# A vision layer in one kernel: softmax sums of two tiles of keys in one pass, with the exponentials added on VectorE

## The chip, the cores and the metric

The kernel runs on one core of one Trainium2 chip. The metric is the time of one execution on the device, in microseconds (us). PE is TensorE, ACT is ScalarE, DVE is VectorE, POOL is GpSimd, SP is SyncE, which here only starts DMAs. PEld is the loading of weights into TensorE.

## The reference, cut to what matters

Sixteen images of 512 x 512 become 1024 tokens each of 256 channels; one layer of attention and one of a mixture of networks follow.

```python
h = tokens(x)                                    # patches @ W + b
q, k, v = split(layernorm(h) @ w_qkv)            # 8 heads of 32
k = sum over f = 1..256 of a_f*sin(f*k) + b_f*cos(f*k)
dots = einsum('bhqd,bhkd->bhqk', q, k) * 32**-0.5
out = einsum('bhqk,bhkd->bhqd', softmax(dots), v)
h = h + out @ w_out + b_out
h = h + networks(layernorm(h))                   # shared MLP + 2 of 4 gated experts
```

All is fp32. The change touches the softmax and the product with `v`.

## The kernel before, in words

The work is cut into rounds. A round makes the transformed keys of four groups of a head pair (the sum over frequencies) and, two rounds behind, one *attention*: two heads against 512 queries, over all 1024 keys. There are 16 images x 4 head pairs x 2 halves of the queries = 128 attentions, each over `NT` = 8 tiles of 128 keys, so 1024 tiles of keys.

For one tile of keys, `kc`:

- **S** (`score`, L1134): two matmuls make the scores of 128 keys against 512 queries for both heads in a PSUM tile `sT` of 128 x 1024 fp32. It comes from the pool `big`, which has two buffers that rotate.
- `exponential` (L1149): ACT takes the exponential from PSUM into an SBUF tile `es`, of which there are `NES` = 5. The big buffer is free after that.
- **W** (`weigh`, L1167): TensorE in four column tiles of 32. Four matmuls multiply `es` with the values `v` (numerators, columns 0 to 255 of the PSUM tile `av`) and four with `ones32`, all ones (denominators, columns 256 to 511). Each matmul leaves two records in the profile. `av` collects over the eight tiles; then `normalize` (L1191 to L1208) takes the reciprocal on DVE, multiplies, and frees `av` for the next attention.

For the keys, SP loads tiles `w` (L951), DVE spreads tiles `f` (L991), POOL multiplies both with integer frequencies (L1006, "turn"), ACT takes sines (L1016), **M** (`mix`, L1036) mixes eight row and column tiles of PE into the second kind of tenant of `big`, `kan`; DVE multiplies it with `f` (L1050, "prod"), and **R** (`add_up`, L1069) adds up. ACT needs one table for sines and another for exponentials, so a round has twelve sines in a row, then eight exponentials, with other small steps between.

Everything else (tokens, norms, keys, queries, values, output projection, networks) is written as four chains of small steps, 0 to 3. A chain's matmul step uses one of two PSUM side banks. The step `values` (L643 to L669) multiplies two tiles of tokens with `wv`; ACT copies the result into the SBUF tile `v`, and for the last head pair into `last`, from where POOL copies it later (`last_values`).

The order of PE's work is written out as strings, `ORDER`: S, M, R, W are the fixed steps, a digit is the next step of that chain. While the program is built, a planner with a cost for each step (`put`, `begin`, `lay_fixed`, `others`) lays the steps of the other engines between: at each point the step that could begin first goes first. The engines then run these queues in order. The strings have 3840 letters; 240 of them make up one image and are repeated eleven times.

Lines that matter: L297 to L306 are the helpers that the chains' matmuls use (L301 whole array, L304 in column tiles, L310 transposes); L548 adds the token bias on DVE; L589 to L599 reduce the angles on DVE, partly in place in PSUM (L594).

Of the kernel before, what the change touches and what calls it, by code (L numbers as in the profile page):

```python
# [11 lines left out]
FP = mybir.dt.float32  # L12
# [6 lines left out]
P = 128  # L19
E = 256  # L20
NPAIR = 4
# [41 lines left out]
KINDS = {"M": "mix", "R": "red", "S": "score", "W": "av"}  # L63
COLUMNS = (128, 32)
ORDER = (
    "333333313133100003000030M0M000MMR3R3M3M",
    "303RMM3MR330M3R3M03MSSRSSWSSWSSWWWW0MWM",
    "WMMRSSSRSWSSWSSW0WWWWMMW3MMRSSRSSWSSWSSW0WW0MMWWWMMRSSRSSWSSWSSW0WWMWWMWMRMSSSWSSWSSWSRW"
    "WWWWMMMMRSSSWSSWSSWSRWWWWW0M0MM0RMS0SSWSSWSWSWSWWW3W3MR13M3MMRSSRSSWSS1SSWWWW3WMWWM3RMS1"
    "SS1SS0SSWWWMS3WR3WWWWM0MMRMS0SS1SR1SSWW1S1SW0W1WW1MMW1W1MM1SSRWSS0SS1WSSWW10RWMWWW1MM10M"  # L70
    "S1SSRWSWR1SS1WSS1W1MMWWMMWW0SS1R1SS1WW1SS1SSW1WRW1WMMW3WMMRS1SS1SW1SS3SSW1WR1WWWWWMM13MM"
    "1RSS0SS0SS0SWWWSWWWR3MMW1WS10S1RSS1S3MMWSS3WRWWSW1WWMW31MM0SS1SSRMS1SSWWWSWR3WWWW3MM131M"
    "S1RSSWWMWSSR3S1S3S1WWW01M1WW1MM0RSS1SWSSWMS1SSWRWW01MW1WWMM101SSRMW1SSWWSS1RSS101MMWWWWW"
    "MS3SSWRMWSS1S01SSW1RW0W3MMWWRWSS131SS1MMWWSS1SSRWWW1WWW101",
    (
        "MM10RMM1SS01SS1SS1WWSS1WWWRWWWMM10MMRS3S1SS1SSWWWSS3RWWWW1W3MM0RMM3SSRSWWWSS1SS1S3WWWMMW"
        "3W311MSRM1WS1S3SWWS3S1SSRW1W0WMM1WWRMM10SS1SS1WW1SS0SSWWRW1WWW0MM10MM1SS1RRWWSS0S1SWSS1W"
        "WWWWMM1S0SRWSSWMMWS1S31SSWRW3WW1WMM3MMR1SS1SS1SSWWWSS1WRWW1WW101"
    )
    * 11,  # L80
    "MM1MM1SSRRWWS1S0SS0SSWWW130MMWW1WRM1MS1",
    "3SSRWWWSS31SS1SW1WWWWMM3RM1S0SSWSS1SSWWMSWR3WWM3WWMM13S1SR1MSWWRS3S1SWS3SWWW01MM1WW10MMR"
    "1SS1SSRWSS1S1WWS0WWWWWMM101MM1SS1RS1SRSSWWWSS01WWMMWWWMS1SSWSSRW0SS1S1WMWWR1WWMM10W1MMR1"
    "SS1SSWWSS1SSWWWR1WM1WW101MM10S1MR1SSWRS1SWSSWS1WWMMWWWRMM1SS0SSWWSSWSSRWWW1WW1M0M1RSS1SS"
    "WSSWSMWSM1WWRWM1W1WMM1RM1SS1SSWWSS1SSWR1W1W1W1MM1WWR1SM1SS1SSWWSSWS1MWWRWMWWM1SS1SWSMSRM"
    "WS1SS1WR1WWW1WW1MM1M1RSS1SWWSS1SSWSWMWW1RW1MM1RW1MM1SSR1SSWWSS1WWSSWWWW1SSSWSSWWSSWSSWWW"
    "W1SS1SS1SWWSSWWWWWW11110110111110000101000100101001000100",
)

@with_exitstack  # L90
def plain_path(ctx: ExitStack, tc: tile.TileContext, a: dict, out: bass.AP, verdict: bass.AP):
# [173 lines left out]
    def begin(engine, deps):  # L265

        if any(d not in done for d in deps):
            return None
        return max([clock[engine]] + [done[d] + LAG for d in deps])
# [138 lines left out]
    def others(limit):  # L408

        soonest = None  # L410
        again = True
        while again:
            again = False
            soonest = None
            for engine in (SP, POOL, ACT, DVE):
                while True:
                    settle()
                    best = min(heads(engine), default=None)
                    chain = min(wanting(engine), default=None)
                    if chain and (  # L420
                        best is None
                        or chain[0] < best[0]
                        or (chain[0] == best[0] and best[2] not in ("prod", "keys"))
                    ):
                        at, lay_it = chain[0], lambda c=chain[1]: step(c)
                    elif best:
                        at, lay_it = best[0], lambda q=best[2]: lay(engine, q)
                    else:
                        break
                    if at > limit:  # L430
                        soonest = at if soonest is None else min(at, soonest)
                        break
                    lay_it()
                    again = True
        return soonest

    def lay_fixed(kind):

        cost, deps, key, action = queues[PE][kind][0]
        user = USERS.get(kind)  # L440
        at = begin(PE, deps + (bigs[-2:-1] if user else []))

        def lay_it():
            queues[PE][kind].pop(0)
            clock[PE] = done[key] = at + cost + retile(TILINGS.get(KINDS[kind]))
            if user:
                bigs.append((user, *key[1:]))
            action()

        return at, lay_it  # L450
# [192 lines left out]
    def values(b):  # L643

        if b > 0:
            yield "av", 2 * NPAIR * b - 3, NT - 1
            yield "all values", b - 1
        last = images[b]["last"] = kup.tile([P, NT, 2, HD], FP, tag="last", name="last")
        for t0 in range(0, NT, 2):
            yield ANY  # L650
            ps = side_tile("v").rearrange("p (t e) -> p t e", t=2)
            for t in range(2):
                for c in range(2):
                    matmul(
                        out=ps[:, t, :],
                        lhsT=hnT[:, c, ts(t0 + t, P)],
                        rhs=wv[:, c, :],
                        start=(c == 0),
                        stop=(c == 1),
                    )  # L660
            yield ACT, 0.62
            src = ps.rearrange("p t (i s d) -> p t i s d", s=2, d=HD)
            for s in range(2):
                nc.scalar.copy(
                    v[:, ds(t0, 2), 0 : NPAIR - 1, ds(HD * s, HD)],
                    src[:, :, 0 : NPAIR - 1, s, :],
                )
            nc.scalar.copy(last[:, ds(t0, 2), :, :], src[:, :, NPAIR - 1, :, :])
        mark("values", b)  # L669

    def last_values(b):
        if b > 0:
            yield "av", 2 * NPAIR * b - 1, NT - 1
        yield POOL, 0.7
        for s in range(2):
            nc.gpsimd.tensor_copy(
                v[:, :, NPAIR - 1, ds(HD * s, HD)], images[b]["last"][:, :, s, :]
            )
        mark("all values", b)

    def gate_weights(ps):
# [463 lines left out]
    def exponential(att, kc):  # L1145
        def action():
            now["table"] = AF.Exp
            es = exps[kc] = esp.tile([P, 1024], FP, tag="es", name="es")
            nc.scalar.activation(es, scores.pop(kc), AF.Exp, scale=SCALE)  # L1149

        deps = [("score", att, kc)]
        old = att * NT + kc - NES
        if old >= 0:
            deps.append(("av", *divmod(old, NT)))
        put(ACT, "fixed", 0.99, deps, ("exp", att, kc), action)

    def weigh(att, kc):

        p = att // 2

        def action():
            if kc == 0:
                acc[0] = avp.tile([P, 512], FP, tag="av", name="av")
            es = exps.pop(kc)
            for half in range(2):
                for i in range(4):
                    nc.tensor.matmul(  # L1167
                        out=acc[0][ts(i, HD), ts(half, 256)],
                        lhsT=ones32 if half else v[:, kc, p % NPAIR, ts(i % 2, HD)],
                        rhs=es[:, ds(512 * (i % 2) + 256 * (i // 2), 256)],  # L1170
                        start=(kc == 0 and half == 0),
                        stop=(kc == NT - 1),
                        skip_group_check=True,
                    )

        deps = [("exp", att, kc)]
        if kc == 0:
            b, i = divmod(p, NPAIR)
            deps.append(("all values" if i == NPAIR - 1 else "values", b))
            if att > 0:  # L1180
                deps.append(("norm", att - 1))
        put(PE, "W", 0.86, deps, ("av", att, kc), action)

    def normalize(att):
        p, qb = divmod(att, 2)
# [44 lines left out]
    def feed(c, *gens):  # L1230
        chains[c]["gens"] += gens

    for name in ("prod", "keys", "norm", "spread"):
        queues[DVE][name] = []
    queues[SP]["source"] = []
    for j in range(XBUFS):
# [33 lines left out]
    for rd in range(B * RI + 2):  # L1270
        groups = range(GS * rd, min(GS * rd + GS, total))
        att = rd - 2
        attends = 0 <= att < ATT
        for g in groups[::2]:
            first = g == groups[0]
            for i, j in ((0, 0), (0, 1), (1, 0), (1, 1), (0, 2), (1, 2)):
                sine(g + i, j, TABLE if first and i == j == 0 else 0.0)
            mix(g)
            mix(g + 1)
            add_up(g // 2)  # L1280

        def table():
            now["table"] = AF.Exp
            nc.scalar.activation(spare[:, 1:2], spare[:, 0:1], AF.Exp)

        put(ACT, "fixed", TABLE + 0.2, [], ("table", rd), table)
        for kc in range(NT) if attends else ():
            score(att, kc)
            exponential(att, kc)
            weigh(att, kc)  # L1290
    with tc.manual_schedule():
        run()
# [746 lines left out]
```

## Time and profile before

| what | value |
|---|---|
| time, median of 3 runs | 3930.66 us (3921.68 to 3933.11) |
| profiled execution, its own time | 3924.07 us |
| its span, from the first to the last instruction | 3922.5 us |
| mean granted TensorE clock | 0.994 |
| busy: PE, PEld | 3810.0, 1948.9 us |
| busy: ACT, POOL, DVE | 3263.0, 3193.6, 2531.7 us |
| DMA | 916.51 MB, mean 234 GB/s |

The profile is one execution. A group of instructions is a line of the kernel, an engine, an operation, and what is written and read (`out<-in`); after the bar come the total busy time in us, the mean of one in ns, and the idle time of the engine just before them with what ended it. A row of waits says which line waited for which, the total in us, how often, and the longest. Matmuls are pipelined and their ends are modelled: the time of one is read from start to start, and a PE that reads as busy can be waiting.

### The profile page before, as it was taken

Reading aid. Unit: us, or ns where it says so; the run is one execution under the profiler, and the core shown is the slowest. Engines: PE = TensorE matmul, PEld = TensorE weight load, DVE = VectorE, ACT = ScalarE, POOL = GpSimd, SP = SyncE. Lnnn points to the kernel's source line nnn. Section 1 sums busy time; section 2 is a strip of 40 time slices with the busy share of each in tenths; the row PEclk is TensorE's granted clock in tenths of the full one; section 3 lists DMA queues with packets and bytes.
Section 4 is the critical chain, followed back from the end, with each engine's and each line's share of the span. In section 5 each row is a group of like instructions: output and inputs, shape, how many; then the busy total and the mean of one; then the engine's idle time right before and its main releaser. Section 6 shows DMA issues by size and latency. Waiting matters only on the chain.

```text
span 3922.5 us, 102737 instructions
## 1 busy us (share of the span) xinstructions
PE 3810.0 (97%) x40337; PEld 1948.9 (50%) x40337; DVE 2531.7 (65%) x4075; ACT 3263.0 (83%) x3939; POOL 3193.6 (81%) x2328
## 2 busy tenths in 40 slices
PE   7899999999999999999999999999999999999998
PEld 4334454554545555455454545545455454544444
DVE  4656757667675766757667675776767767576652
ACT  2788888888888888888888888888888888888983
POOL 3998878788788878879788788878879888888860
PEclk9999999999999999999999999999999999999999
DMA  7987968888787888979889788798878889788860
GB/s 228 281 261 217 278 192 245 259 226 258 220 257 225 237 264 224 259 216 256 235 233 265 212 257 247 224 265 224 262 218 255 247 229 265 216 245 235 221 170 18
DMA packets 587615, 916.51 MB, mean 234 GB/s; under 512 B 58828, under 2 KB 177524, under 8 KB 587124
## 3 DMA queue, kind: packets, MB, share of 16 engines
q1 hardware_dynamic: 580880, 906.98, 80.6%
q8 instruction: 321, 5.26, 0.6%
q10 hardware_dynamic: 6244, 2.88, 0.3%
q14 instruction: 170, 1.39, 0.1%
HBM read 758.64 MB, written 150.99 MB: 232 GB/s over the span
## 4 chain that ended last, share of the span: by engine, by line
PE 66%; DMA 13%; ACT 8%; POOL 5%; DVE 4%; issue 3%; SPq 2%; ACTq 0%; POOLq 0%; DVEq 0%
PE av L1167 17%; PE sT L1134 10%; PE kan L1036 8%; DMA w<-ud 7%; PE red L1069 4%; PE e1p L301 3%; PE tok L301 3%; ACT w L1016 3%; POOL w L1006 3%; PE e3p L301 2%; PE tok L304 2%; DMA k<-kd 2%; PE s1p L301 2%; PE e1p L304 2%; ACT f L1016 2%
## 5 line engine op out<-in xcount | busy, mean ns | idle before, releaser
L1006 POOL TENSOR_TENSOR w<-w,lane 128x1024 int32<-128x1024 int32 x1024 | 1923.6, 1895 | 406.9 <-DMA w<-ud 275.7
L1149 ACT ACTIVATE es<-sT 128x1024 f32<-128x1024 f32 x1024 | 1014.3, 1022 | 357.3 <-PE sT L1134 312.2
L1016 ACT ACTIVATE w<-w 128x1024 f32<-128x1024 int32 x1024 | 1013.4, 1046 | 67.5 <-POOL w L1006 64.3
L1006 POOL TENSOR_TENSOR f<-f,lane 128x1024 int32<-128x1024 int32 x512 | 970.2, 1895 | 102.0 <-DVE f L991 84.8
L1134 PE MATMUL sT<-q,k 128*128 128x512 f32 x2048 | 707.6, 454 | 42.9 <-DMA k<-kd 13.4
L1050 DVE TENSOR_TENSOR f<-kan,f 128x1024 f32<-128x1024 f32 x512 | 605.2, 1214 | 203.1 <-ACT f L1016 116.3
L991 DVE STREAM_SHUFFLE f<-src 128x1024 int32<-128x1024 int32 x512 | 681.3, 1370 | 0.4
L1167 PE MATMUL av<-es,v 128*32 128x256 f32 x8192 | 638.8, 383 | 3.5 <-DVE rc L1208 2.6
L1167 PE MATMUL av<-es,ones 128*32 128x256 f32 x8192 | 630.9, 379 | 0.0
L1036 PE MATMUL kan<-w,coef 64*32 64x512 f32 x8192 | 540.1, 598 | 18.8 <-ACT w L1016 12.6
L1016 ACT ACTIVATE f<-f 128x1024 f32<-128x1024 int32 x512 | 519.0, 1046 | 4.1 <-POOL f L1006 4.1
L1134 PEld LDWEIGHTS sT<-q,k 128*128 128x128 f32 x2048 | 351.2, 190 | 340.0 <-issue 146.0
L1167 PEld LDWEIGHTS av<-es,v 128*32 128x32 f32 x8192 | 235.5, 109 | 343.2 <-issue 236.9
L1167 PEld LDWEIGHTS av<-es,ones 128*32 128x32 f32 x8192 | 267.2, 110 | 176.4 <-issue 1.4
L1191 DVE RECIPROCAL rc<-av 128x256 f32<-128x256 f32 x128 | 224.8, 1756 | 169.5 <-PE av L1167 169.5
L1036 PEld LDWEIGHTS kan<-w,coef 64*32 64x32 f32 x8192 | 129.1, 105 | 313.9 <-issue 133.4
L1069 PE MATMUL red<-f,pack 128*32 128x512 f32 x2048 | 271.0, 602 | 0.0
L301 PE MATMUL tok<-wt,x 128*128 128x256 f32 x768 | 182.1, 389 | 22.1 <-DMA w1s<-in_sW 12.5
L1016 ACT ACT_TABLE_LOAD x128 | 164.2, 1283 | 17.7 <-DMA w<-ud 15.5
L304 PE MATMUL tok<-wt,x 128*32 128x256 f32 x3072 | 178.0, 380 | 0.6 <-DVE h L548 0.6
L301 PEld LDWEIGHTS tok<-wt,x 128*128 128x128 f32 x768 | 147.4, 194 | 57.9 <-DMA w1s<-in_sW 12.4
L513 ACT ACTIVATE hn<-h,less,rstd 128x256 f32<-128x256 f32 x256 | 140.7, 591 | 39.8 <-POOL less L505 39.0
(148 smaller groups left out, 4269.5 us busy)
## 6 DMA issues: line engine op xcount, KB each, us to landing
w<-ud SPq DMA_DIRECT2D x2048, 256.0 KB
q<-qd SPq DMA_DIRECT2D x512, 128.0 KB
k<-kd SPq DMA_DIRECT2D x128, 512.0 KB
x<-in_xT SPq DMA_DIRECT2D x128, 384.0 KB
ud<-u SPq DMA_DIRECT2D x64, 512.0 KB
ud<-ui SPq DMA_DIRECT2D x64, 512.0 KB
src<-ud SPq DMA_DIRECT2D x512, 64.0 KB
qd<-qhi SPq DMA_DIRECT2D x64, 256.0 KB
```

Source lines behind the costliest of these rows:

```text
L301: nc.tensor.matmul(out=out, lhsT=lhsT, rhs=rhs, start=start, stop=stop)
L304: nc.tensor.matmul(out=out[ts(i, 32)], lhsT=lhsT[:, ts(i, 32)], rhs=rhs, start=start, stop=stop)
L991: nc.vector.stream_shuffle(w, sources[g // 8].rearrange("p r n -> p (r n)"), [4 * (g % 8) + i // 8 for i in range(32)],)
L1006: nc.gpsimd.tensor_tensor(w, w, f.to_broadcast([P, N]), ALU.mult)
L1016: nc.scalar.activation(x, w, AF.Sin, scale=TURN * 2.0**-32)
L1036: nc.tensor.matmul(out=ps[ds(64 * j + 32 * blk, 32), ts(r, 512)], lhsT=coef[ts(r, 64)].rearrange("p e f j -> p (e f j)"), rhs=w[ts(r, 64), ...
L1050: nc.vector.tensor_mul(w, kan.pop(g), w)
L1069: nc.tensor.matmul(out=rows_of_pair[p][ts(2 * i + r, 32), :], lhsT=pack[:, ds(PACK0 - 16 * (k % 2) - 2 * (k // 2), 32)], rhs=prod[:, ts(r, ...
L1134: nc.tensor.matmul(out=ps[:, ts(s, 512)], lhsT=k4[:, 2 * s + kc // 4, ts(kc % 4, P)], rhs=q4[:, s, :], start=True, stop=True,)
L1149: nc.scalar.activation(es, scores.pop(kc), AF.Exp, scale=SCALE)
L1167: nc.tensor.matmul(out=acc[0][ts(i, HD), ts(half, 256)], lhsT=ones32 if half else v[:, kc, p % NPAIR, ts(i % 2, HD)], rhs=es[:, ds(512 * ( ...
L1191: nc.vector.reciprocal(rc[0], acc[0][:, 256:512])
```

## The change

For an even and the following odd tile of keys, with exponentials e0 and e1 and values v0 and v1, the product e0 v0 + e1 v1 is written as e0 (v0 - v1) + (e0 + e1) v1, and the denominators need e0 + e1 alone.

- `exponential`: an even tile still goes to an SBUF tile `es`. An odd tile's exponential is written in place, into its PSUM tile.
- `pair_sum`, new: DVE adds the PSUM tile of the odd one and the SBUF tile of the even one into a new `es` tile, `both`. This frees the odd tile's big buffer, so `lay_fixed` makes the S or M that takes that buffer next wait for the sum.
- `weigh`: an even tile is multiplied with the values alone (four matmuls, not eight); an odd one takes `both`, with values and with ones.
- `values`: of each two tiles of tokens ACT copies the second, and DVE subtracts it from the first. `last` has another shape, and `last_values` copies once.
- The planner has a new DVE queue, "sum", named first; `ORDER` is another string with the same number of each letter.

```diff
@@ ORDER: the repeated part, 240 letters @@
-        "MM10RMM1SS01SS1SS1WWSS1WWWRWWWMM10MMRS3S1SS1SSWWWSS3RWWWW1W3MM0RMM3SSRSWWWSS1SS1S3WWWMMW"
-        "3W311MSRM1WS1S3SWWS3S1SSRW1W0WMM1WWRMM10SS1SS1WW1SS0SSWWRW1WWW0MM10MM1SS1RRWWSS0S1SWSS1W"
-        "WWWWMM1S0SRWSSWMMWS1S31SSWRW3WW1WMM3MMR1SS1SS1SSWWWSS1WRWW1WW101"
+        "MM0R1MM1S1SS1SSW1S0S1SRWW0WWWWMM1MMRS3SS1SS1SSWWRSWWWWW3W13MM0RMM3SSS1SSWRWWS1SSWW3WMW3"
+        "WM311MRSM1SWSSS1WR3SS31SWW0WW1WM1MW1MM0SS1SRW1SWS0S1WSSWRWWWWM01MM10RM0SS1SW1SSWW1SSWRS1"
+        "WWWWMM1MS0SSWRWMSW1S1SS3SWWRW3WW1MM31MMRS1SS1WWSS1SS1SWWRWWWW101"
...
@@ others @@
-                        or (chain[0] == best[0] and best[2] not in ("prod", "keys"))
+                        or (chain[0] == best[0] and best[2] not in ("sum", "prod", "keys"))
@@ lay_fixed @@
         user = USERS.get(kind)
+        if kind == "S" and key[2] % 2:
+            user = "sum"
@@ values @@
-        last = images[b]["last"] = kup.tile([P, NT, 2, HD], FP, tag="last", name="last")
+        last = images[b]["last"] = kup.tile([P, NT, 2 * HD], FP, tag="last", name="last")
...
-            yield ACT, 0.62
-            src = ps.rearrange("p t (i s d) -> p t i s d", s=2, d=HD)
-            for s in range(2):
-                nc.scalar.copy(
-                    v[:, ds(t0, 2), 0 : NPAIR - 1, ds(HD * s, HD)],
-                    src[:, :, 0 : NPAIR - 1, s, :],
-                )
-            nc.scalar.copy(last[:, ds(t0, 2), :, :], src[:, :, NPAIR - 1, :, :])
+            held = chains[now["chain"]]["bank"]
+            yield ACT, 0.5
+            chains[now["chain"]]["bank"] = held
+            homes = (
+                (v[:, :, 0 : NPAIR - 1, :].rearrange("p t i d -> p t (i d)"), slice(0, 192)),
+                (last, slice(192, 256)),
+            )
+            for home, part in homes:
+                nc.scalar.copy(home[:, t0 + 1, :], ps[:, 1, part])
+            yield DVE, 0.6
+            for home, part in homes:
+                nc.vector.tensor_sub(home[:, t0, :], ps[:, 0, part], home[:, t0 + 1, :])
@@ last_values @@
-        for s in range(2):
-            nc.gpsimd.tensor_copy(
-                v[:, :, NPAIR - 1, ds(HD * s, HD)], images[b]["last"][:, :, s, :]
-            )
+        nc.gpsimd.tensor_copy(v[:, :, NPAIR - 1, :], images[b]["last"])
@@ exponential @@
-            es = exps[kc] = esp.tile([P, 1024], FP, tag="es", name="es")
-            nc.scalar.activation(es, scores.pop(kc), AF.Exp, scale=SCALE)
+            ps = es = scores[kc]
+            if kc % 2 == 0:
+                es = exps[kc] = esp.tile([P, 1024], FP, tag="es", name="es")
+            nc.scalar.activation(es, ps, AF.Exp, scale=SCALE)
...
+    def pair_sum(att, kc):
+        def action():
+            both = exps[kc] = esp.tile([P, 1024], FP, tag="es", name="both")
+            nc.vector.tensor_add(both, scores[kc], exps[kc - 1])
+
+        deps = [("exp", att, kc - 1), ("exp", att, kc)] + tile_free(att, kc)
+        put(DVE, "sum", 1.16, deps, ("sum", att, kc), action)
@@ weigh @@
-            es = exps.pop(kc)
-            for half in range(2):
+            es = exps[kc]
+            for half in range(1 + kc % 2):
...
-        deps = [("exp", att, kc)]
+        deps = [("sum" if kc % 2 else "exp", att, kc)]
...
-        put(PE, "W", 0.86, deps, ("av", att, kc), action)
+        put(PE, "W", 0.86 if kc % 2 else 0.43, deps, ("av", att, kc), action)
@@ plain_path @@
-    for name in ("prod", "keys", "norm", "spread"):
+    for name in ("sum", "prod", "keys", "norm", "spread"):
...
+            if kc % 2:
+                pair_sum(att, kc)
```

More of the change, by code (lines that the diff above doesn't have):

```diff
@@ L65 @@
 ORDER = (
[L66 to L72, printed above, removed]
@@ L73 @@
-    "S1RSSWWMWSSR3S1S3S1WWW01M1WW1MM0RSS1SWSSWMS1SSWRWW01MW1WWMM101SSRMW1SSWWSS1RSS101MMWWWWW"
-    "MS3SSWRMWSS1S01SSW1RW0W3MMWWRWSS131SS1MMWWSS1SSRWWW1WWW101",
-    (
-        "MM10RMM1SS01SS1SS1WWSS1WWWRWWWMM10MMRS3S1SS1SSWWWSS3RWWWW1W3MM0RMM3SSRSWWWSS1SS1S3WWWMMW"
-        "3W311MSRM1WS1S3SWWS3S1SSRW1W0WMM1WWRMM10SS1SS1WW1SS0SSWWRW1WWW0MM10MM1SS1RRWWSS0S1SWSS1W"
-        "WWWWMM1S0SRWSSWMMWS1S31SSWRW3WW1WMM3MMR1SS1SS1SSWWWSS1WRWW1WW101"
+    "333333313133100003300M00M00R00MM0MR3M33",
+    "RM3M33MR03MR303MMSS0WSSWRWSSS3S03WWMMWW",
@@ new lines @@
+    "RMWMSSSRSSSWWSSWWW3WMM0RM0WWSSSSSSSWWWSMWWWRM0WMMWMRSSSSWWSSSRWSWWWWMMWMRMSSWSSSSWSSWRW0"
+    "MWMMWMWWSSSRSSWWSWRSWSWWWW0M00M0SSSWRMWSWS3SW3SMSWRW3WMWM3MRMSS1SSWSSWRSSWW3W3MMWWWMR1SS"
+    "S0SSWWS3S1MSWR1WM30MWWWSWM1R01SM1WS1WWSS1RSS1S0W1W1WWWMM0RMSSS1SSW1SWSW1SMW1RWMWW01MMWM1"
+    "SS1RSRSWWS1SS0S1W1MMWMMWRSWWWS1S1S0SS1WWS1S3RWW1WMW1M1WMMWSS1SRSS1RS1SWWW1SW31WWMMW3WM0S"
+    "SR0S1S0SWWSS1SMW3RM1W0WMMW1RWMWSS1S3SS1SSWWRS31WWWWWWM103MS1SSW1WSRS3MSWWSSMW1WWRWM13MM1"
+    "S3SSRMSWWS3WSS3R1SW0WWM1WM1W1RM0SS1SW1SSWSSWWSMW1W1RM0M1WW1MS1S1MRWS1SWRSWS0SS1WM1WMWWWS"
@@ L79 @@
+    "S0RM3S1WMS1SWWSS0SWRW3WW10MMW31MS1SS1WRSSW1MS1SSWWWRW1WW01",
+    (
+        "MM0R1MM1S1SS1SSWW1S0S1SRWW0WWWWMM1MMRS3SS1SS1SSWWRSWWWWW3W13MM0RMM3SSS1SSWRWWS1SSWW3WMW3"
+        "WM311MRSM1SWSSS1WR3SS31SWW0WW1WM1MW1MM0SS1SRW1SWS0S1WSSWRWWWWM01MM10RM0SS1SW1SSWW1SSWRS1"
+        "WWWWMM1MS0SSWRWMSW1S1SS3SWWRW3WW1MM31MMRS1SS1WWSS1SS1SWWRWWWW101"
     )
     * 11,
-    "MM1MM1SSRRWWS1S0SS0SSWWW130MMWW1WRM1MS1",
-    "3SSRWWWSS31SS1SW1WWWWMM3RM1S0SSWSS1SSWWMSWR3WWM3WWMM13S1SR1MSWWRS3S1SWS3SWWW01MM1WW10MMR"
@@ L83 @@
[L83 to L87, printed above, removed]
+    "MM10RMS3SS1SS01SSWWWSM1RWWWW1WMM01MS1MR",
+    "WSS1SS3WWSS3WRSWW1WW30MM1RMS1SS3SS1SWWSSWMW3RMM311WMWMWWSRSSR3S1SSWWWS13S0WW1WWMMW1M01MS"
@@ L88 @@
+    "1S1SSRRSW1SW1SSWW101WMWWMWMMRSSS1SSW1WS1RWSSWWW1MM1WMSWSSR0SSWW1MS1SW1W1S10RW1MMWWW0MRMS"
+    "1SS1SS1SSWW1SWR0WW1W1WMMMW1SRSS1SSWW1MSWSWS1WR1MMWWWRMS1S0SWMS1SSWSRSW0WWWWW10M1M1SS0RSS"
+    "MWWSSS1SMWWR1MWW1MW1WR1MMS1SWS1SWSWSS1SRWWW1WWMMR1M1MSS1SW1SS1SWSSWRWW1M1WW1MMMWSSSRSSWS"
+    "SRWWS1WWWMMRWW1MM1SS1W1S1SWSSS1SRWW1WWMWM1WM1MRS1RSWS1SWSS1SSWWWW1WW1SS1WS1SS1SSWWWSSWWW"
+    "W1SS1S1SWSWSSWWWWWW11110110111110101001000000101001000100",
 )
@@ L1147, in action, with tile_free @@
             now["table"] = AF.Exp
-            es = exps[kc] = esp.tile([P, 1024], FP, tag="es", name="es")
-            nc.scalar.activation(es, scores.pop(kc), AF.Exp, scale=SCALE)
-        deps = [("score", att, kc)]
-        old = att * NT + kc - NES
-        if old >= 0:
-            deps.append(("av", *divmod(old, NT)))
-        put(ACT, "fixed", 0.99, deps, ("exp", att, kc), action)
+            ps = es = scores[kc]
+            if kc % 2 == 0:
+                es = exps[kc] = esp.tile([P, 1024], FP, tag="es", name="es")
+            nc.scalar.activation(es, ps, AF.Exp, scale=SCALE)
+        deps = [("score", att, kc)] + (tile_free(att, kc) if kc % 2 == 0 else [])
+        put(ACT, "fixed", 0.99, deps, ("exp", att, kc), action)
+    def tile_free(att, kc):
+        old = att * NT + kc - NES
+        if old < 0:
+            return []
+        deps = [("av", *divmod(old, NT))]
+        return deps if old % 2 else [*deps, ("sum", *divmod(old + 1, NT))]
+    def pair_sum(att, kc):
[4 more added lines that the diff above has]
+        put(DVE, "sum", 1.16, deps, ("sum", att, kc), action)
     def weigh(att, kc):
```

## The prediction

> **What bounds the kernel now.** I read the page first: the span, the busy shares and the chain that ended last.
>
> ```profile
> span 3922.5 us, 102737 instructions
> ...
> PE 3810.0 (97%) x40337; PEld 1948.9 (50%) x40337; DVE 2531.7 (65%) x4075; ACT 3263.0 (83%) x3939; POOL 3193.6 (81%) x2328
> ...
> PE 66%; DMA 13%; ACT 8%; POOL 5%; DVE 4%; issue 3%; SPq 2%; ACTq 0%; POOLq 0%; DVEq 0%
> ```
>
> PE is busy for 97%, and two thirds of the chain are PE's; VectorE (DVE) has the most room. Then the busy time by stages, in stretches of 500 us:
>
> ```profile
> core 0: us, PE busy (x) PEld busy (x) DVE busy (x) ACT busy (x) POOL busy (x), PEclk, DMA share, GB/s
> 2000.00:2500.00 500.00, 496.65 (x5359) 260.99 (x5361) 339.32 (x541) 432.01 (x522) 425.78 (x308) 1.00 0.86 243
> 3000.00:3500.00 500.00, 495.94 (x5460) 254.57 (x5452) 343.96 (x546) 432.71 (x526) 425.90 (x311) 1.00 0.83 241
> ```
>
> In the steady part PE is at 99%, ACT 86%, POOL 85%, the DMA engines 83 to 86%, DVE 68%. But ends of matmuls are modelled, so 99% hides waits. The timeline of PE shows what a pass really takes:
>
> ```profile
> 2005.22 0.64 PE L1167 MATMUL av<-es,v 128*32 128x256 f32 x8
> 2005.68 0.61 PE L1167 MATMUL av<-es,ones 128*32 128x256 f32 x8
> 2006.11 0.61 PE L1167 MATMUL av<-es,v 128*32 128x256 f32 x8
> 2006.54 0.61 PE L1167 MATMUL av<-es,ones 128*32 128x256 f32 x8
> 2006.97 0.61 PE L1167 MATMUL av<-es,v 128*32 128x256 f32 x8
> 2007.41 0.61 PE L1167 MATMUL av<-es,ones 128*32 128x256 f32 x8
> 2007.95 1.21 PE L1134 MATMUL sT<-q,k 128*128 128x512 f32 x4
> ```
>
> From start to start a pass over one tile, with values or with ones, takes 0.432 us, not 0.61; the step to an S takes 0.54, so the change of tiling costs 0.11. With such prices (S 0.45, M and R 0.86, W 0.86, a digit step 0.1 to 1.72 by what it multiplies) PE's whole order sums to 3250 us, and 1091 changes of tiling add 120: well under 3922. The rest is the start, the end, and waits. So a PE pass taken out is only worth its time if no new wait stands in its place. The waits of PE's weight loads:
>
> ```profile
> PEld kan L1036 <- ACT w L1016: 105.4, 184, 3.7
> PEld sT L1134 <- ACT es L1149: 74.8, 136, 2.2
> PEld sT L1134 <- DVE f L1050: 52.9, 94, 3.1
> ```
>
> The last two are S waiting for one of the two big PSUM tiles, which rotate among S and M. That is the resource the change holds longer.
>
> **The change part by part.** The profiled execution took 3924.07 us (span 3922.5); the median of the three runs is 3930.66, 6.6 more. I make the sum against 3924. About 0.3%, 12 us, is what a measurement of this kernel can tell from no change.
>
> *Passes of ones.* There were 1024, one per tile of keys; 512 remain: 512 x 0.432 = 221 us of PE, on the path: **-221**.
>
> *The new order.* Counted over the whole strings with digits left out, neighbours of unlike tiling (S; W and R; M) go from 1091 to 1205: 114 x 0.11 = **+12** (0 to 25, since digits lie between many of them).
>
> *The sum on DVE.* 512 additions of a PSUM tile and an SBUF tile, 128x1024. The groups of instructions hold the same form, L1050's product:
>
> ```profile
> L1149 ACT ACTIVATE es<-sT 128x1024 f32<-128x1024 f32 x1024 | 1014.3, 1022 | 357.3 <-PE sT L1134 312.2 <-PE av L1167 43.2 <-PE lnT L310 1.0
> L1050 DVE TENSOR_TENSOR f<-kan,f 128x1024 f32<-128x1024 f32 x512 | 605.2, 1214 | 203.1 <-ACT f L1016 116.3 <-PE kan L1036 72.2 <-ACT es L1149 9.6
> L594 DVE SCALAR_TENSOR_TENSOR k<-u,k 128x512 f32<-128x512 int32 x128 | 89.0, 695 | 3.8
> L598 DVE TENSOR_SCALAR u<-k 128x512 f32<-128x512 f32 x64 | 43.7, 683 | 0.7
> L548 DVE TENSOR_TENSOR h<-tok,tokb 128x256 f32<-128x256 f32 x128 | 54.1, 423 | 117.8 <-PE tok L301 81.7 <-PE tok L304 34.4
> ```
>
> So 512 x 1.214 = 622 us of DVE. With the subtractions below DVE goes to 2532 + 622 + 37 = 3190, 82% of 3900: not the bound, and off the path as throughput. As latency it is on it, next.
>
> *The big tile of an odd tile of keys is held longer.* Now the loop is S, exponential, next S but one. The timeline of both engines:
>
> ```profile
> 2028.72 0.73 PE L1134 MATMUL sT<-q,k 128*128 128x512 f32 x2
> 2029.55 1.02 ACT L1149 ACTIVATE es<-sT 128x1024 f32<-128x1024 f32 x1 [0.43 <-PE sT L1134]
> ```
>
> 0.83 us from the start of S to its exponential, 1.02 for it, and 0.05 at the shortest handover in the trace: 1.90. After, an odd tile adds 0.06 and 1.21 for the sum: 3.18 from S to the S (or M) two big tiles later. In that time PE has only what the order puts between. Of 511 such handovers the commonest, 83 times, is S, one step of chain 1, S: 0.45 + 0.45 + 1.72 for a step of two 512-column products = 2.62, short by 0.56. Next, 18 times, W and S: short by 1.5. I added up the shortfalls of all S and M in both orders: 43 us before, 287 after, so +244. With 0.15 more per digit step for its change of tiling it is 34 and 242, +208; with 0.30, 28 and 206, +178. I take the middle: **+209**. The bounds are 178 and 244. The measured waits of S now (128 us in the rows above) are about 90 more than the 34, from queues at ACT and DVE; that part is in the 3924 already. If DVE is busy when the exponential ends, each handover grows: with 0.4 us more (a third of a shuffle of 1.37 or a product) the shortfalls are 356, **0 to +114**. I take 0, since the planner lets the sum go first among DVE's fixed steps.
>
> Behind a waiting sum stand on DVE products, keys, shuffles and normalizations, and for these wait M, POOL's turns and the first W of the next attention; they are covered as long as DVE has its 18%.
>
> *What the new waits replace.* PE waits 105 us for sines (row above) and 13 more at the matmuls themselves. While an S stalls, POOL and ACT go on towards the next sines, so some of this goes: 0 to -118. ACT must still finish eight exponentials before the next twelve sines, which speaks for little: **-30**, a quarter.
>
> *Exponentials in PSUM.* No ACT row writes PSUM. DVE in place in PSUM takes 695 ns (L594) against 683 into SBUF (L598), 2%: +20 ns. ACT's exponential, which reads PSUM, takes 1022 against 1046 of the sine, which reads SBUF: -24 ns. Over 512 that is between -12 and +10 us of ACT, at 83%; I take 0. [...]
>
> *Values as difference and second.* 64 times ACT makes two copies (192 and 64 columns) in place of three of 0.28 to 0.32: some 23 us less ACT. DVE gets two subtractions, by L548 some 0.36 and 0.22: 64 x 0.58 = 37. The side bank is held about 0.6 longer, 38 us if PE stood still each time; the other side bank and the other chains cover it: 0. POOL makes one copy in place of two, under 10 us, off the path.
>
> The sum: 3924 - 221 + 12 + 209 - 30 = 3894. Runs lie a little above the profiled one, so I say **3900**.
>
> **The rivals.**
> - *Most of the gain is kept.* The order leaves stalls where PE would have waited for sines or loads anyway: all 118 go, and the shortfall is the low bound. 3924 - 209 + 178 - 118 = 3775. For it: PE was the chain's main part. Against: the waits for sines come after the exponentials on ACT, not in their place.
> - *Nothing measurable.* Stalls equal the saving: 3924 - 209 + 209 = 3924.
> - *Slower: the rotation of the two big tiles bounds.* DVE's queue adds its 0.4 us to each odd handover: 3924 - 209 + 322 = 4037 (356 less 34). It decides as soon as new stalls exceed 209 us, 0.41 per pair of tiles. For it: S waits already more than its floor. Against: DVE still has a fifth of its time free.
> - *Exponentials into PSUM are slow*, far beyond the rows: at twice the time ACT gets 520 us more and becomes the bound: 4100 and above. No row points there.
>
> **How the numbers follow.** Forecast, 3840 to 3917: 0.37; gain kept: 0.15; nothing: 0.12; rotation, 3940 to 4080: 0.32; slow exponentials: 0.04. So faster 0.52, same 0.12, slower 0.36. The range from 3800 to 4010 leaves out half of the second case and a third of the fourth, and the last.
>
> **What would show it.** Right: the ones group at 4096 records instead of 8192; a DVE group of 512 at about 1.21 us; waits of S for DVE's sum of some 200 us, new, as the largest of PE's; PE busy down by about 200; ACT's exponentials still near 1.02. Wrong: S waiting under 100 us for the sum (then it is 3775), or far over 209 (then slower); exponentials of odd tiles well over 1.1 us.

## The result: 1.1% slower, and the profile after

| | before | after |
|---|---|---|
| time, median | 3926.69 us of 4 (3921.68 to 3933.11) | 3970.30 us of 4 (3964.42 to 3981.68) |
| ratio, 95% interval | | 1.0114 [1.0083, 1.0144] |
| profiled execution, its span | 3924.07, 3922.5 us | 3981.68, 3980.1 us |
| mean granted TensorE clock | 0.994 | 0.982 |

The time lies inside the range, but on the other side of zero: slower by 44 us in the medians, and by 57.6 us between the two profiled executions. What is read from the traces below refers to the 57.6. The page after, first the busy shares, then the groups that the change made or touched:

```profile
PE 3728.6 (94%) x35701; PEld 1810.7 (45%) x35701; DVE 3113.4 (78%) x4715; ACT 3259.1 (82%) x3875; POOL 3191.7 (80%) x2312
...
L1169 DVE TENSOR_TENSOR both<-sT,es 128x1024 f32<-128x1024 f32 x512 | 624.4, 1220 | 314.5 <-ACT sT L1154 301.2
L1154 ACT ACTIVATE sT<-sT 128x1024 f32<-128x1024 f32 x512 | 517.4, 1011 | 272.0 <-PE sT L1137 203.7
...
L1154 ACT ACTIVATE es<-sT 128x1024 f32<-128x1024 f32 x512 | 521.4, 1018 | 131.2 <-PE sT L1137 120.4
...
L1184 PE MATMUL av<-both,ones 128*32 128x256 f32 x4096 | 320.4, 384 | 0.0
```

The change did what it says. The ones have 4096 records instead of 8192, the sum takes 1220 ns, and an exponential that ends in PSUM takes 1011 ns against 1018 into SBUF. But PE's busy time fell by 81 us only, from 3810.0 to 3728.6, though 221 us of passes are gone. The waits of PE's weight loads and then of its matmuls (line that waits, line waited for: us in all, times, longest):

```profile
PEld sT L1137 <- ACT es L1154: 171.3, 221, 3.6
...
PEld kan L1039 <- ACT w L1019: 121.9, 198, 6.1
...
PEld sT L1137 <- DVE both L1169: 104.1, 99, 4.5
PEld sT L1137 <- DVE f L1053: 79.4, 111, 4.3
```

```profile
PE sT L1137 <- DVE both L1169: 57.3, 58, 4.1
PE sT L1137 <- ACT es L1154: 49.7, 68, 3.2
...
PE sT L1137 <- DVE f L1053: 20.3, 36, 3.4
PE kan L1039 <- ACT w L1019: 19.2, 13, 5.2
```

The two lists must not be added. Where PE stands still, the wait is mostly in both of them, longer for the loads and shorter for the matmuls behind them, as at this S:

```profile
2000.45 0.30 PEld L1137 LDWEIGHTS sT<-q,k 128*128 128x128 f32 x2 [0.95 <-DVE f L1053]
2000.45 0.73 PE L1137 MATMUL sT<-q,k 128*128 128x512 f32 x2 [0.52 <-DVE f L1053]
```

The six rows of S add up to 482 us, but the idle stretches behind them cover 357. The matmuls' rows before, to go with those of the loads in the prediction, are:

```profile
PE sT L1134 <- ACT es L1149: 12.7, 25, 1.8
PE kan L1036 <- ACT w L1016: 12.6, 13, 3.2
PE sT L1134 <- DVE f L1050: 7.2, 11, 2.2
```

By the weight loads, S waits 104 us for the new sum, about half of the forecast's sign of being right (some 200). It also waits longer for exponentials (171 against 74.8) and for products (79 against 52.9): 355 us in the three rows against 128 before, **227 more**. By the matmuls it is 127 against 20, 107 more. The loads' rows read long, since earlier matmuls can still be running (0.95 us at the S above, where the matmul behind reads 0.52); the matmuls' rows rest on modelled ends. The sines, from which I had taken 30 us off, rose from 105 to 122 at the loads.

A single handover of an odd tile, in the timeline of its engines:

```profile
2006.95 0.73 PE L1137 MATMUL sT<-q,k 128*128 128x512 f32 x2
...
2007.78 1.01 ACT L1154 ACTIVATE sT<-sT 128x1024 f32<-128x1024 f32 x1
...
2008.82 1.23 DVE L1169 TENSOR_TENSOR both<-sT,es 128x1024 f32<-128x1024 f32 x1 [2.06 <-ACT sT L1154]
...
2010.10 0.73 PE L1137 MATMUL sT<-q,k 128*128 128x512 f32 x2
```

0.83 us to the exponential, 1.04 to the sum, 1.28 to the next S in this buffer: 3.15 us, where I had built 3.18 from rows of before. Of the 511 odd handovers in the trace, 224 end within 0.2 us of the sum's end and so bind the next S; before, 55 of 511 ended so behind their exponential.

Busy time by stretches (the columns of the page: PE, PEld, DVE, ACT, POOL with their counts, then granted clock, DMA share, GB/s), to be held against the table of before:

```profile
0.00:500.00 500.00, 414.49 (x3659) 186.47 (x3663) 344.50 (x522) 338.51 (x389) 377.66 (x262) 0.93 0.80 239
2000.00:2500.00 500.00, 480.18 (x4701) 239.77 (x4701) 403.26 (x611) 428.43 (x511) 418.92 (x297) 0.99 0.83 236
3000.00:3500.00 500.00, 478.87 (x4657) 238.45 (x4654) 407.51 (x620) 422.66 (x502) 414.92 (x296) 0.99 0.83 239
```

In the steady part PE falls from 99% to 96%, DVE rises from 68% to 81%, and no engine reads as full. An image takes 238.1 us there against 236.2 (mean of the fourth to the thirteenth). Where the 57.6 us arise is seen from the ends of the images' attentions (us; the last check of an image's sums, L1219 before and L1236 after):

| image | 1 | 2 | 3 | 13 | 16 |
|---|---|---|---|---|---|
| before | 357.7 | 599.2 | 845.1 | 3207.4 | 3860.5 |
| after | 389.2 | 619.5 | 859.4 | 3240.8 | 3918.5 |
| later by | 31.5 | 20.3 | 14.3 | 33.4 | 58.0 |

The first image's attentions end 31.5 us later, at a granted clock of 0.93 in the first 500 us against 0.98 before, but more than half of that is made up by the third. The ten images after it lose 19 us, and the last three 25.

### The profile page after: what moved, and what is told of

Its sections match the earlier page's. It is cut to its first block, busy times and chain, and to the rows that moved or that the text cites. A ratio compares the mean times of both kernels' runs of the same rounds, so it can differ in the third digit from the quotient of the medians.

```text
span 3980.1 us, 93620 instructions
## 1 busy us (share of the span) xinstructions
PE 3728.6 (94%) x35701; PEld 1810.7 (45%) x35701; DVE 3113.4 (78%) x4715; ACT 3259.1 (82%) x3875; POOL 3191.7 (80%) x2312
## 5 line engine op out<-in xcount | busy, mean ns | idle before, releaser
L1009 POOL TENSOR_TENSOR w<-w,lane 128x1024 int32<-128x1024 int32 x1024 | 1924.5, 1894 | 397.2 <-DMA w<-ud 255.5
L1009 POOL TENSOR_TENSOR f<-f,lane 128x1024 int32<-128x1024 int32 x512 | 969.9, 1894 | 111.2 <-DVE f L994 105.2
L1137 PE MATMUL sT<-q,k 128*128 128x512 f32 x2048 | 750.5, 466 | 170.2 <-DVE both L1169 57.3
L1169 DVE TENSOR_TENSOR both<-sT,es 128x1024 f32<-128x1024 f32 x512 | 624.4, 1220 | 314.5 <-ACT sT L1154 301.2
L1154 ACT ACTIVATE sT<-sT 128x1024 f32<-128x1024 f32 x512 | 517.4, 1011 | 272.0 <-PE sT L1137 203.7
L994 DVE STREAM_SHUFFLE f<-src 128x1024 int32<-128x1024 int32 x512 | 687.0, 1359 | 0.4
L1154 ACT ACTIVATE es<-sT 128x1024 f32<-128x1024 f32 x512 | 521.4, 1018 | 131.2 <-PE sT L1137 120.4
L1184 PE MATMUL av<-both,v 128*32 128x256 f32 x4096 | 325.5, 389 | 3.9 <-DVE both L1169 3.5
L1184 PE MATMUL av<-es,v 128*32 128x256 f32 x4096 | 323.9, 387 | 3.5 <-DVE rc L1225 3.4
L1184 PE MATMUL av<-both,ones 128*32 128x256 f32 x4096 | 320.4, 384 | 0.0
L301 PE MATMUL tok<-wt,x 128*128 128x256 f32 x960 | 225.7, 386 | 16.4 <-DMA w1s<-in_sW 13.2
L301 PEld LDWEIGHTS tok<-wt,x 128*128 128x128 f32 x960 | 180.6, 192 | 73.0 <-issue 20.4
L1184 PEld LDWEIGHTS av<-es,v 128*32 128x32 f32 x4096 | 110.7, 109 | 197.3 <-issue 155.6
L1184 PEld LDWEIGHTS av<-both,v 128*32 128x32 f32 x4096 | 114.9, 110 | 168.7 <-issue 96.3
```

The costliest lines, as they stand in the source:

```text
L301: nc.tensor.matmul(out=out, lhsT=lhsT, rhs=rhs, start=start, stop=stop)
L994: nc.vector.stream_shuffle(w, sources[g // 8].rearrange("p r n -> p (r n)"), [4 * (g % 8) + i // 8 for i in range(32)],)
L1009: nc.gpsimd.tensor_tensor(w, w, f.to_broadcast([P, N]), ALU.mult)
L1137: nc.tensor.matmul(out=ps[:, ts(s, 512)], lhsT=k4[:, 2 * s + kc // 4, ts(kc % 4, P)], rhs=q4[:, s, :], start=True, stop=True,)
L1154: nc.scalar.activation(es, ps, AF.Exp, scale=SCALE)
L1169: nc.vector.tensor_add(both, scores[kc], exps[kc - 1])
```

## The experiments

Three theories stood at the start. **Handover**: the removed passes are worth about their time, and the longer hold of the odd tile's buffer eats it. **Load**: DVE's new 624 us delay everything else on it. **Order**: a fixed order of PE loses or wins for reasons of its own. Each time below is a median, with its ratio to the kernel before run on the same chip.

**1. The odd tile's exponential into SBUF.** The kernel after, with the buffer released by ACT as before.

```diff
-            ps = es = scores[kc]
-            if kc % 2 == 0:
-                es = exps[kc] = esp.tile([P, 1024], FP, tag="es", name="es")
-            nc.scalar.activation(es, ps, AF.Exp, scale=SCALE)
+            es = exps[kc] = esp.tile([P, 1024], FP, tag="es", name="es")
+            nc.scalar.activation(es, scores.pop(kc), AF.Exp, scale=SCALE)
...
-            both = exps[kc] = esp.tile([P, 1024], FP, tag="es", name="both")
-            nc.vector.tensor_add(both, scores[kc], exps[kc - 1])
+            nc.vector.tensor_add(exps[kc], exps[kc], exps[kc - 1])
```

> Changed kernel, but the odd tile's exponential goes to an SBUF tile too and VectorE adds the two SBUF tiles in place, so a big PSUM tile is free after its exponential as before the change; TensorE's and VectorE's work and the order are those of the changed kernel. Theory H (the hold of the big tile through the sum makes S wait): the waits of S fall from some 480 us back to about 150, and the time to 3924 - 209 = 3715, with some 50 for what comes late next: 3720 to 3790. Theories O (the new order itself) and D (VectorE's 622 us delay products and normalizations): S's waits may fall, but the time stays at 3940 to 3980.

The 480 and 150 us in this text are both lists of waits added; at the loads alone they are 355 and 128.

4252.56 us, 1.083 [1.0812, 1.0848]. It was no clean test, as its groups of instructions show:

```profile
L1007 POOL TENSOR_TENSOR w<-w,lane 128x1024 int32<-128x1024 int32 x1024 | 2150.9, 2116 | 206.0 <-DMA w<-ud 141.0 <-PE s1p L301 17.6 <-PE sT L1135 8.8
...
L1164 DVE TENSOR_TENSOR es<-es 128x1024 f32<-128x1024 f32 x512 | 987.6, 1931 | 259.5 <-ACT es L1150 257.2
```

The same sum with both operands in SBUF takes 1931 ns instead of 1220, and POOL's turns of `w` 2116 in the mean instead of 1894. The trace after has the like: its sums from PSUM took 1219 ns where a POOL instruction ran beside them (486 of the 512) and 1221 where none did, but a product of two small SBUF tiles (L704, 128x16) took 1078 ns in the mean beside POOL (18 of 32) and 175 where none of its instructions ran. Adding from PSUM was thus the cheaper form here; that POOL is what lengthened the other one is inferred from these numbers and was not tested alone. The hold had to be tested in another way.

**2. Passes alone.** The kernel before, with ones on odd tiles only; denominators lack the even tiles. PE's order stays, and the planner lays the other engines' steps with the new price.

```diff
-            for half in range(2):
+            for half in range(1 + kc % 2):
...
-        put(PE, "W", 0.86, deps, ("av", att, kc), action)
+        put(PE, "W", 0.86 if kc % 2 else 0.43, deps, ("av", att, kc), action)
```

> Kernel before, in its own order, with the ones taken in the odd tiles of keys alone and nothing put in their place: the denominators lack the even tiles' exponentials. It prices the first term by itself. If TensorE's passes are worth their time: 3924 - 221 = 3703. If the other engines and the DMAs, at 84 to 86 per cent in the steady part, take over: 3780 to 3860. Theory H expects under 3800, since nothing is held longer here.

3889.37 us, 0.9909 [0.9893, 0.9926]. **In this order the 221 us of passes were worth 37.** A lower granted clock (0.989 against 0.994 in the profiled executions) may hide some 20 more, not the rest. The waits of its weight loads tell where the rest went:

```profile
PEld kan L1036 <- ACT w L1016: 185.4, 283, 3.7
...
PEld sT L1134 <- ACT es L1149: 106.1, 167, 3.2
PEld sT L1134 <- DVE f L1050: 84.3, 125, 3.1
```

Against 105.4, 74.8 and 52.9 before, 143 us more in the three rows. PE reaches the same sines, exponentials and products sooner and waits for them.

**3, 4. The orders exchanged.** The kernel before with the new `ORDER`, and the kernel after with the old one; only the strings differ.

> Kernel before with the changed kernel's order string and nothing else. Theory H: the order costs its 114 more changes of tiling, 12 us, and some spacing: 3925 to 3950. Theory O: the order, above all its first part, loses the 30 us that the first image took longer, and more: 3965 and above.

> Changed kernel with the order string of before. Theory H: the old order puts single steps between the S of a pair and the next, so the held tile is waited for at least as often: 3970 to 4100, S's waits at 480 us or more. Theory O: without the new order the time falls under 3950.

4055.54 us, 1.0324 [1.0307, 1.0341], and 4264.73 us, 1.0865 [1.0845, 1.0885]. Either order fits only its own kernel. So the new order is not a cost of 12 us beside the rest, and an experiment that keeps an order while it changes steps also measures a misfit.

**5. Passes alone in the new order.** Experiment 2 with the new `ORDER`: no sum, no longer hold.

> Kernel before with the ones in odd tiles alone (denominators lack the even tiles) and the changed kernel's order: TensorE's passes and order are those of the changed kernel, but no sum, no held tile, no new values. Theory H: what the changed kernel loses against this is the hold, so this is well under the 3970 of the changed kernel, by the forecast's shortfall of some 200: 3770 to 3860. Theory B (the engines are so balanced that a pass taken out of TensorE is worth little in any order, as the 37 of 221 us in the old order suggests): 3890 to 3950.

3993.20 us, 1.0168 [1.0145, 1.0191]: slower than the complete change in the same order, though it does less. Its weight loads wait 189.4 us for exponentials at S. The misfit is as large as the effects that I wanted to tell apart.

**6, 7. A short sum, then VectorE's load back.** The kernel after, with the odd exponential in SBUF and DVE adding only 64 of its 1024 columns from the buffer, so that the next S waits for a short operation; then a maximum over 1024 columns on DVE whose result nobody uses. Denominators and the product of a pair are incomplete in both.

```diff
-            both = exps[kc] = esp.tile([P, 1024], FP, tag="es", name="both")
-            nc.vector.tensor_add(both, scores[kc], exps[kc - 1])
+            few_of = exps[kc][:, 0:64]
+            nc.vector.tensor_add(few_of, scores[kc][:, 0:64], few_of)
...
+        def load_vector():
+            nc.vector.tensor_reduce(few[:, 6:7], exps[kc], AX.X, ALU.max)
+
+        put(DVE, "sum", 1.1, [("sum", att, kc)], ("more", att, kc), load_vector)
```

> Changed kernel, but the odd tile's exponential goes to SBUF and VectorE adds only 64 of the 1024 columns, from the big tile (the sum of the other columns is left out): the big tile is still freed by VectorE, but some 1.0 us earlier, and VectorE has 512 us less. Theory H: the handover falls from 3.2 to 2.2 us, S's waits to 200 or so, the time to 3840 to 3890. Theory B: 3900 to 3950.

> As the run with the short hold (64 of 1024 columns added), and behind each such sum VectorE takes a maximum over the odd tile's 1024 columns in SBUF, about 1.1 us, whose result nothing uses: VectorE's load is again about that of the changed kernel, the hold stays short. Theory H: within 30 us of the short hold. Theory D (VectorE's 622 us delay its products, and so the big tiles, anyway): back to 3940 to 3990.

4001.21 us, 1.0200 [1.0183, 1.0217], and 4052.52 us, 1.0326 [1.0309, 1.0344]. The load costs 51 us. The first number, above the kernel after, again has the misfit of an order laid for something else.

**8. The values as before.** The kernel after with the old copies in `values` and `last_values` (three by ACT, two by POOL, no subtraction); the first tile of a pair then keeps its own values in place of the difference.

> Changed kernel with the values step of before (three ACT copies per two tiles, no difference taken, so the even tiles' products use the wrong values). All theories but one put it within 15 us of the changed kernel, 3955 to 3985; if the subtractions and the longer hold of the side bank cost something, it is under 3950.

3964.14 us, 1.0106 [1.0089, 1.0123], against 1.0114 for the change. The intervals of the two ratios overlap, so no cost of the values can be measured.

**9 to 11. An order laid anew for each kernel.** For the kernel before, for the kernel after and for the passes alone the strings were searched again in one and the same way against the planner's own times, with prices nearer to the trace: S's handover 0.33 longer (0.83 from S to its exponential in the trace, against 0.47 for S in the planner), 0.13 more between a chain's matmul step and its next, and the sum at 1.22.

```diff
-            clock[PE] = done[key] = at + cost + retile(TILINGS.get(KINDS[kind]))
+            clock[PE] = at + cost + retile(TILINGS.get(KINDS[kind]))
+            done[key] = clock[PE] + (0.33 if kind == "S" else 0.0)
...
-            ch["ready"] = clock[PE] = at + took
+            clock[PE] = at + took
+            ch["ready"] = clock[PE] + 0.13
```

> Kernel before, same work, with another order, searched for it by moving letters, and with the planner reckoning the handover from S to its exponential 0.33 us later and from other matmul steps 0.13 us later, as the trace shows them. It is the control for the two others of this call. Expected by all theories: a little faster, 3880 to 3925.

> Changed kernel, same work, with an order searched anew for it in the same way, and the same two handovers (and 1.22 us for the sum) in the planner. Theory L (the changed kernel lost because its order was laid with handovers too short, and its loops are three long where they were two): it falls under the replanned control, to 3800 to 3880. Theory H (the hold and the sum take back what the passes bring, in any order): it stays level with the replanned control or above, 3890 to 3950, though below 3970.

> Kernel before with the ones in odd tiles alone (denominators lack the even tiles), order searched for it in the same way, same handovers in the planner. It prices the saved passes in an order that fits them. Theory H: 150 to 200 of the 221 us come out against the control, 3700 to 3770, and what the changed kernel lies above it is the price of hold and sum. Theory B (the other engines cap the gain): 3820 and above.

Before: 3964.59 us, 1.0088 [1.0059, 1.0118]. After: 4033.67 us, 1.0260 [1.0226, 1.0294]. Passes alone: 3824.08 us, 0.9740 [0.9711, 0.9769]. The new strings are worse than the two originals, by 34 us and, between ratios, by some 57, so the idea that the change only suffers from handovers priced too short found no support. But among the three, laid alike, the comparison is fair: **the passes are worth 140 us (3964.6 − 3824.1) once the order is fitted to them, and the sum with all that hangs on it costs 210 (4033.7 − 3824.1)**. The two kernels of the 140 have the same granted clock (0.992 for the passes alone, 0.991 for the kernel before); against the original kernel before, in its own order, the passes are worth 107. The waits of the passes-alone kernel, weight loads:

```profile
PEld kan L1036 <- ACT w L1016: 122.4, 184, 3.6
PEld sT L1134 <- ACT es L1149: 93.0, 116, 3.4
...
PEld sT L1134 <- DVE f L1050: 61.7, 99, 1.8
```

and those of the kernel after, replanned:

```profile
PEld sT L1137 <- ACT es L1154: 163.4, 167, 5.0
PEld kan L1039 <- ACT w L1019: 150.7, 237, 4.0
...
PEld sT L1137 <- DVE f L1053: 105.8, 136, 4.0
PEld sT L1137 <- DVE both L1169: 90.8, 113, 3.3
```

**12, 13. The 210 us taken apart.** Experiments 6 and 7 with orders laid in the same way.

> The short hold (sum of 64 of 1024 columns from the big tile, the other columns left out) with an order searched for it in the same way as for the three replanned kernels before. Between the replanned half ones (3824) and the replanned changed kernel (4034) lie 210 us; this has the new wait of S for VectorE in the handover, but 1.0 us shorter, and almost no load on VectorE. If the length of the sum, as hold or as load, is what costs: 3840 to 3900. If the mere wait for a third engine costs: 3930 and above.

> The short hold with a maximum over 1024 columns in SBUF on VectorE behind each short sum, whose result nothing uses, order searched for it in the same way: VectorE's load is that of the changed kernel, the hold is short. Theory H (the hold of the big tile): within 30 us of the short hold alone. Theory D (VectorE's load delays its other steps): within 40 us of the replanned changed kernel, 3990 to 4040. Half and half: 3930 to 3970.

3954.26 us, 1.0059 [1.0036, 1.0081], and 3997.86 us, 1.0173 [1.0149, 1.0198]. The kernel before was 3 us slower in this batch than in the last, so the steps are taken between ratios: from the passes alone (0.9740) to a short sum 3.2%, some 125 us; to the load 1.1%, some 45; to the full sum and hold 0.9%, some 34 (DVE has 70 us less to do there, 3201.8 against 3132.2). The granted clock of the four profiled executions is 0.992, 0.983, 0.984 and 0.972; the share that is missing, times the span, is 31, 67, 64 and 113 us. If PE was the bound in all of that time, the clock made up to 37 us of the first step, nothing of the second and all of the third. The short sum takes 0.22 us itself:

```profile
L1167 DVE TENSOR_TENSOR es<-sT,es 128x64 f32<-128x64 f32 x512 | 113.0, 221 | 451.1 <-ACT es L1152 450.7
```

and yet S waits for it, and longer for products than in the passes-alone kernel (weight loads):

```profile
PEld sT L1137 <- DVE f L1053: 140.1, 184, 3.2
...
PEld sT L1137 <- DVE es L1167: 87.5, 110, 2.5
PEld sT L1137 <- ACT es L1152: 62.1, 84, 4.1
```

So the largest part is not the length of the sum, and it is larger than what the clock can explain. It comes with making a buffer's release, and the pass over the odd tile, wait for a third engine at all: S, then ACT, then DVE, then S. This kernel differs from the passes alone also in the values (no cost measured in experiment 8). Every search was finite, so the split holds between comparably laid orders and not for the best possible ones; its sizes are good to perhaps the 34 us by which the replanned kernel before missed the original.

## Why the prediction was wrong, step by step

- **The failing step: "512 x 0.432 = 221 us of PE, on the path: −221".** The size of a pass was right, "on the path" was not. Alone, in the old order, the passes brought 37 us; in an order laid for them 140. The text itself had said that a pass "is only worth its time if no new wait stands in its place", had summed PE's order to 3370 us with tilings, far under 3922, and then counted new waits only where the sum made them. The missing waits are those of experiment 2: sines, exponentials and products, all from engines that were 65 to 83% busy and whose work did not shrink. PE's two thirds of the chain did not make all of a pass's time PE's to give. With 140 in place of 221 and every other term as forecast the sum reads 3975, a loss instead of a gain.
- **The handover, "+209": the size came out, its make-up did not.** One odd handover takes 3.15 us (3.18 forecast), and between kernels laid alike the sum with all that hangs on it costs 210. That these agree is in part luck. The forecast put it all on the length of the hold, with S waiting some 200 us for the sum; its loads wait 104. With the hold some 1 us shorter, experiment 12 still pays 125 us. In the rest are DVE's load, which was taken as 0, and perhaps a lower granted clock (82 of the 210 us at most, 0.972 against 0.992). The sign "under 100 us for the sum (then it is 3775)" was nearly met by a kernel that became slower. The rival with the rotation of the two big tiles, given 0.32, is the only case whose times (3940 to 4080) hold the result. Its rule, that it decides as soon as the new stalls exceed 209 us, stays open: S's waits grew by 227 at the loads and by 107 at the matmuls.
- **"If DVE is busy when the exponential ends": 0 taken of 0 to +114.** Experiments 7 and 13 put the load at 51 and 45 us. Inside the bounds, but the point taken was the lower end. In the trace after, 167 of the 512 sums begin more than 0.1 us behind their exponential, and the mean over all is 0.29 us; 86 of them found a shuffle running (L994, 1.36 us). That the sum is laid first among DVE's fixed steps did not help these.
- **"−30" for sines that the stalls replace**: the loads' wait for them rose from 105 to 122 us. The sign was wrong. The text had a reason beside it: sines follow the exponentials on ACT, so what delays an exponential delays them too; no run tested this alone. Its "13 more at the matmuls" were no more: they lie inside the 105, so the bound of 118 was 105.
- **Not thought of: the granted clock.** Stretches at half speed add up to 141 us after and 45 before. In the trace after, the matmuls of 512 columns that make `q` (L301) start 0.853 us apart in these stretches and 0.429 outside (medians), so PE does half as much there and the 96 us more are worth 48 at most, if PE was the bound in all of them. How much of it was really paid was not separated.
- **The order, "+12"**: cannot be told apart; the misfits of experiments 3 and 4 show that an order is not an item with a price of its own.
- **Right**: exponentials into PSUM at 0 (1011 against 1018 ns, 0.7% shorter each); the values at 0 (no cost found in experiment 8); the sum's duration (1.220 against 1.214 us).

What stays open: why the first image ends 31.5 us late and the last three lose 25. The clock is lowest in the first stretch (0.93), and at both ends the order is not the repeated one, but no experiment changed only these stretches.

## What to carry to other kernels

Here every engine was 65 to 97% busy around a fixed order, and work taken from the busiest one was not its time saved (37 or 140 of 221 us). In such a kernel take it out in a throw-away kernel first, once in the old order and once in an order laid for it, and read which waits grow. A buffer that a third engine has to release cost here some 125 us by the extra link in the chain, though that engine's operation took 0.2 us; count the queue in front of that operation as well as its length. A shared order has to be laid anew for both sides of every comparison, otherwise its misfit (129 us in experiment 3) hides the effect. And the waits of weight loads and of matmuls are two views of the same stalls; read one or the other, not their sum.

## What the runs showed of the chip

- **The granted clock often fell after short gaps.** After, PE's starts lie more than 2.5 us apart in 29 places; in 23 of them a stretch at half clock begins 2.5 to 5.2 us behind the first of the two starts, and before in 7 of 10. Most stretches last 3.4 or 6.8 us (27 of the 29, and 8 of 9 before). Six of the 29 stretches after follow no such gap, so the gap alone does not decide it. In one place before, PE stands 2.35 us (between starts: 1900.1 and 1902.9 us), and the windows around it are (clock in the third column from the right):

```profile
1900.00:1903.00 3.00, 0.65 (x4) 0.28 (x3) 2.88 (x10) 2.98 (x4) 0.22 (x1) 1.00 1.05 229
1903.00:1907.00 4.00, 4.00 (x7) 2.01 (x8) 0.19 (x3) 2.12 (x3) 2.26 (x2) 0.57 1.07 273
1907.00:1910.00 3.00, 3.00 (x29) 1.35 (x28) 2.93 (x6) 1.03 (x1) 2.35 (x3) 1.00 1.07 356
```

  The middle window reads 0.57: half speed for some 3.4 of its 4.0 us. Before has 9 stretches at half speed, after 29. In this place a gap of 2.35 us came before the stretch. By an estimate from these rows, a wait of 3 to 5 us, as the longest ones of S and M after (3.2 to 5.2 us at the matmuls), can cost some 1.7 us more, half of a stretch of 3.4, if such a stretch follows and PE is the bound in it.
- **An addition of two SBUF tiles and POOL's turns both took longer in one kernel**: 1931 ns against 1220 from PSUM, and 2116 against 1894 (experiment 1).
- **An exponential in place in PSUM cost no more** than one into SBUF: 1011 against 1018 ns (trace after).
